# A four-layer graph network on one core: the rows between layers 1 and 2 are stored in another order, and the gathers of layer 3 get a small clear behind each

## The chip, the cores and the metric

The kernel runs on one core of one Trainium2 chip. The metric is the device time of one execution in microseconds (us), as the median of the runs shown. Engines are called PE (TensorE; PEld is its weight load), DVE (VectorE), ACT (ScalarE), POOL (GpSimd) and SP (the sync engine, which here only issues DMAs). L936 is line 936 of the kernel.

## What is computed

The graph has N = 2708 nodes with 128 features each, and a dense 2708 x 2708 matrix `adj` that is mostly zero (a row has some 16 entries). Four layers follow each other, each with a residual and a layer norm:

```
x = layernorm(x + (adj.T @ x) / adj.sum(axis=0))                    # layer 0
m = gelu(s[i] + d[j] + b);  agg[i] = sum_j adj[i, j] * m            # layer 1
x = layernorm(x + layernorm(gelu([x, agg] @ U.T + u) + x) * w + b)
h = adj @ (x @ W) + b                                               # layer 2
x = layernorm(x + leaky(gamma * batchnorm(h) + beta))
for each of 4 heads:                                                # layer 3
    s = exp(8 * tanh((leaky(x1[i] + x2[j]) @ a) / 8)) * adj
    out = leaky((s / s.sum(-1)) @ x @ Wlin.T)
x = layernorm(x + concat(out) @ w)
```

## The kernel before

The kernel works with lists of neighbours instead of the dense matrix. Nodes are taken in 22 blocks of 128 (21 full blocks and one of 20).

**Up to about 203 us.** SP loads the rows of `adj` into a ring of nine slots (`ring`, L338, tile `rows`, 10.8 KB in each partition). PE sums layer 0, DVE extracts each row's neighbours, and the rows are ranked by their number of neighbours. `rank[i]` is the place of node i in that order and `perm[r]` is the node at place r. Lists and layer-0 rows are written to DRAM in rank order by scatters on POOL (L255, an indirect DMA that takes its row numbers from a column of indices).

**Layer 1, about 203 to 1021 us.** The loop at L1035 takes the 22 blocks in rank order. `messages` (L865) gathers, for each neighbour slot of a block, 128 rows of 512 bytes from `d_dram` (`gather`, L247: one indirect DMA on POOL for each column of indices). Up to eight gathers fill one `msg` tile, of which there are five. DVE adds a term (L896), ACT applies gelu (L899) and DVE sums the weighted rows (L882, L884). `update` (L906) makes the block's new rows `x_n`; the last step of that is L321. Rows of a block lie in rank order, so L936 scatters them by `perm` into `x2_dram`, which is thereby in node order. Beside this, PE transposes `adj` into `at_dram` (L944, ACT L974, SP L976). From the twelfth block on, `layer2` (L1001) gathers 128 rows of `at_dram` by `perm` into a ring slot (tile `at_rows`, 1.35 MB each, L1005) and PE sums layer 2 (L1014, L1018).

**Between the layers, about 1021 to 1112 us.** The pools of layers 1 and 2, the ring among them, are closed at the end of the `with` at L337. The pools `ready` and `bn` (L1097, L1099) are then laid out in the same memory. SP loads `x2_dram` into the tile `x2` (L1103, L1104). DVE forms batch norm (L1121 to L1145), makes masks for layer 3 (`masks`, L1150, whose first instructions are iotas on POOL, L1147, L1155, L1157), and from L1185 on normalises; L1190 adds `x2`. The rows of the table `t2_dram` (644 floats a row) are written by SP.

**Layer 3, about 1112 to 1912 us.** Neighbour lists are cut into 100 groups of four columns ("quads"). `fetch` (L1531) gathers four times up to 128 rows of 2576 bytes from `t2_dram` into a tile `g4`, of which there are nine (`GOT`, L82). In each quad PE repeats and adds rows (L1358, L1364), DVE computes scores (L1556, L1557, L1374, L1382), and ACT sums them (L1390). Two quads are closed together (`rest`, L1395), and with PE's L1436 their `g4` tiles come free. Finished rows are scattered by POOL to the output (L1512). In this layer PE, DVE and ACT run in the order in which the code is written; POOL's and SP's order, and in layers 1 and 2 nearly everybody's, is set by a scheduler that works with estimated times. `tc.issue_after(i)` puts an instruction behind `i` in the order of its engine, without a wait.

Of the kernel before, what the change touches and what calls it, by code (L numbers as in the profile page):

```python
# [1 line left out]

# [7 lines left out]
FP = mybir.dt.float32  # L10
# [5 lines left out]
P = 128  # L16
N = 2708
D = 128
NFULL = N // P
NREM = N - NFULL * P  # L20
NBLK = NFULL + 1
# [7 lines left out]
I8 = mybir.dt.int8  # L29
# [30 lines left out]
RING = 9  # L60
LW = 2 * SLOTS + 2
BLOCKS = [(b * P, min(P, N - b * P)) for b in range(NBLK)]
# [23 lines left out]
def gnn_resnorm_kernel(  # L86
# [21 lines left out]
    nc = tc.nc  # L108
# [98 lines left out]
    keep = ctx.enter_context(tc.tile_pool(name="keep", bufs=1))  # L207
# [9 lines left out]
    x2_dram = tables.tile([NBLK * P, D], FP, name="x2_dram")  # L217
# [3 lines left out]
    t2_dram = tables.tile([NBLK * P, RW], FP, name="t2_dram")  # L221
    ls = keep.tile([P, NBLK, LW], FP, name="ls")
    idx = keep.tile([P, NBLK, SLOTS], I32, name="idx")
    perm = keep.tile([P, NBLK], I32, name="perm")
# [5 lines left out]
    idx3 = keep.tile([P, CHUNK3[NB3]], I32, name="idx3")  # L230
    val3 = keep.tile([P, CHUNK3[NB3]], FP, name="val3")
    rank = keep.tile([P, NBLK], I32, name="rank")
# [6 lines left out]
    ones = keep.tile([P, P], FP, name="ones")  # L239
    nc.gpsimd.memset(ones, 1.0)  # L240

    def natural(dram, b0, b1):

        return dram[b0 * P : b1 * P, :].rearrange("(b p) w -> p b w", p=P)

    def gather(dst, table, index):
        nc.gpsimd.indirect_dma_start(  # L247
            out=dst,
            out_offset=None,
            in_=table[0:N, :],  # L250
            in_offset=bass.IndirectOffsetOnAxis(ap=index, axis=0),
        )

    def scatter(table, index, rows):
        return nc.gpsimd.indirect_dma_start(  # L255
            out=table,
            out_offset=bass.IndirectOffsetOnAxis(ap=index, axis=0),
            in_=rows,
            in_offset=None,
        ).ins  # L260
# [69 lines left out]

    graph = ExitStack()
    own_ps = graph.enter_context(tc.tile_pool(name="own_ps", bufs=1, space=PSUM))

    def banks(name):
        return [bank.tile([P, 512], FP, name=f"{name}{i}", tag="bank") for i in range(6)]

    with ExitStack() as layer:  # L337
        ring = layer.enter_context(tc.tile_pool(name="ring", bufs=RING))  # L338
        work = layer.enter_context(tc.tile_pool(name="work", bufs=1))
        small = layer.enter_context(tc.tile_pool(name="small", bufs=2))  # L340
        engine = mybir.EngineType
# [312 lines left out]
        for g in KINDS:  # L654
            j = 32 // g
# [250 lines left out]
        def update(b, x_s, x_st, parts):  # L906
            n = BLOCKS[b][1]
            tp = tail_ps.tile([P, 512], FP, name="tail")
            for i in range(2):
                nc.tensor.matmul(  # L910
                    tp[:, 0:n], lhsT=parts[0:n, i, :], rhs=ident[0:n, 0:n],
                    start=(i == 0), stop=(i == 1),
                )
            x_b = mine.tile([P, D], FP, name="x_b")
            nc.vector.tensor_tensor(x_b[0:n], x_s[0:n, 1, :], lnb[0:n], ALU.add)
            agg_t = mine.tile([P, P], FP, name="agg_t")
            nc.scalar.copy(agg_t[:, 0:n], tp[:, 0:n])
            pn = tp[0:n, P : 2 * P]
            nc.tensor.matmul(pn, lhsT=x_st[:, 0:n], rhs=u1_t, start=True, stop=False)
            nc.tensor.matmul(pn, lhsT=ones[0:1, 0:n], rhs=updb[0:1, :], start=False, stop=False)  # L920
            nc.tensor.matmul(pn, lhsT=agg_t[:, 0:n], rhs=u2_t, start=False, stop=True)
            new = mine.tile([P, 1, D], FP, name="new")
            x_n = mine.tile([P, 1, D], FP, name="x_n")
            sums = mine.tile([P, 2], FP, name="sums1")
            h, s0, s1 = new[0:n, 0, :], sums[0:n, 0:1], sums[0:n, 1:2]
            nc.scalar.activation(h, pn, AF.Gelu)
            nc.vector.scalar_tensor_tensor(
                h, h, 1.0, x_s[0:n, 1, :], ALU.mult, ALU.add, accum_out=s0
            )
            rstd = deviation(mine, n, 1, new[0:n], s0)  # L930
            nc.vector.scalar_tensor_tensor(h, h, s0, lnw[0:n], ALU.add, ALU.mult)
            nc.vector.scalar_tensor_tensor(
                h, h, rstd[0:n, 0:1], x_b[0:n], ALU.mult, ALU.add, accum_out=s1
            )
            normalised(mine, n, 1, new[0:n], s1, x_n[0:n])
            scatter(x2_dram, perm[0:n, b : b + 1], x_n[0:n, 0, :])  # L936
            nc.tensor.transpose(tp[:, 256 : 256 + n], x_n[0:n, 0, :], ident[0:n, 0:n])
            x_nt = mine.tile([P, P], FP, name="x_nt")
            nc.scalar.copy(x_nt[:, 0:n], tp[:, 256 : 256 + n])
            px = tp[0:n, 384:512]  # L940
            nc.tensor.matmul(px, lhsT=x_nt[:, 0:n], rhs=w2_l2, start=True, stop=True)
            nc.scalar.copy(xw[0:n, b, :], px)
# [92 lines left out]
        for i, b in enumerate(TURNS):  # L1035
# [10 lines left out]
            for _ in range(2 if i < 1 else 1):  # L1046
                if left:
                    e = left.pop(0)
# [15 lines left out]
            for _ in range(2 if i in (9, 10, 11) else 1):  # L1064
                if i and again:
                    e = again.pop(0)
# [3 lines left out]
            if i >= 11:  # L1070
                for k in range(2 * (i - 11), min(i, 2 * (i - 10))):
                    layer2(k)
        layer2(NBLK - 1)

# [21 lines left out]
    with ExitStack() as layer:  # L1098
        work = layer.enter_context(tc.tile_pool(name="bn", bufs=1))  # L1099
        small = layer.enter_context(tc.tile_pool(name="bn_small", bufs=2))  # L1100
        hb = work.tile([P, NBLK, D], FP, name="hb")
        x2 = work.tile([P, NBLK, D], FP, name="x2")
        nc.sync.dma_start(x2[:, 0:NFULL, :], natural(x2_dram, 0, NFULL))  # L1103
        nc.sync.dma_start(x2[0:NREM, NFULL, :], x2_dram[NFULL * P : N, :])  # L1104
        a_all = keep.tile([P, HEADS, D], FP, name="a_all")
        nc.scalar.dma_start(a_all, att.partition_broadcast(P))
        w1_sb = keep.tile([P, HEADS, D], FP, name="w1_s")
# [75 lines left out]
        for b0, count, n in quads():  # L1183
            h = hb[0:n, b0 : b0 + count]
            nc.vector.tensor_tensor(h, h, broad(scale, n, count), ALU.mult)  # L1185
            nc.vector.tensor_tensor(h, h, broad(beta_row, n, count), ALU.add)
            nc.vector.scalar_tensor_tensor(h, h, 0.2, h, ALU.mult, ALU.max)
            sums = small.tile([P, 4], FP, name="sums2")
            for j in range(count):
                nc.vector.scalar_tensor_tensor(  # L1190
                    hb[0:n, b0 + j, :], hb[0:n, b0 + j, :], 1.0, x2[0:n, b0 + j, :],
                    ALU.mult, ALU.add, accum_out=sums[0:n, j : j + 1],
                )
            normalised(
                small, n, count, h, sums[0:n, 0:count], xs[0:n, b0 : b0 + count, :],
                newton=False,
            )
            w = (count - 1) * P + n
            nc.sync.dma_start(
                t2_dram[b0 * P : b0 * P + w, HD : HD + D].rearrange("(b p) w -> p b w", p=n),  # L1200
                xs[0:n, b0 : b0 + count, :],
            )
            for b in range(b0, b0 + count):
                did = scatter(x3_dram, rank[0:n, b : b + 1], xs[0:n, b, :])
                for before in sent:
                    tc.declare_no_dep(
                        did, before, query=mybir.DependencyQuery.ANY_SYNC,
                        reason="each row has a place of its own",
                    )
                sent.append(did)  # L1210
            pt = bank.tile([P, 512], FP, name="pt_x3", tag="bank")
            for j in range(count):
                nc.tensor.transpose(
                    pt[:, j * P : j * P + n], xs[0:n, b0 + j, :], ident[0:n, 0:n]
                )
            xt = small.tile([P, 512], FP, name="xt3")
            nc.scalar.copy(xt[:, 0:w], pt[:, 0:w])
            for j in range(count):
                at = slice(j * P, j * P + n)
                pm = bank.tile([P, 512], FP, name="pm_t", tag="bank")  # L1220
                nc.tensor.matmul(pm[0:n], lhsT=xt[:, at], rhs=w2_sb, start=True, stop=True)
                pa = bank.tile([P, 512], FP, name="pa_t", tag="bank")
                nc.tensor.matmul(
                    pa[0:n, 0:HEADS], lhsT=xt[:, at], rhs=w_a2, start=True, stop=True
                )
                row = small.tile([P, HD], FP, name="t_row", bufs=4)
                nc.scalar.copy(row[0:n], pm[0:n])
                beta_t = small.tile([P, HEADS], FP, name="beta_t", bufs=4)
                nc.vector.tensor_copy(beta_t[0:n], pa[0:n, 0:HEADS])
                r0 = (b0 + j) * P  # L1230
                nc.sync.dma_start(t2_dram[r0 : r0 + n, 0:HD], row[0:n, :])
                nc.sync.dma_start(t2_dram[r0 : r0 + n, HD + D : RW], beta_t[0:n, :])
# [6 lines left out]
    with ExitStack() as layer:  # L1239
# [291 lines left out]
        def fetch(i):  # L1531
            b, j = quads[i]
            e = BLOCKS3[b][0] * (P // BLOCKS3[b][0])
            g4 = got.tile([P, 4, RW], FP, name="g4")
            for r in range(4):
                ch = CHUNK3[b] + 4 * j + r
                gather(g4[0:e, r, :], t2_dram, idx3[0:e, ch : ch + 1])
            gathered[i] = g4

        fetch(0)  # L1540
# [1 line left out]
        for i, (b, j) in enumerate(quads):  # L1542
            g, jj = BLOCKS3[b]
            e = g * (P // g)
# [553 lines left out]
```

## Time and profile before

| what | us |
|---|---|
| median of 3 runs (lowest, highest) | 1938.81 (1932.17, 1943.18) |
| the profiled execution | 1931.8 |
| its span | 1930.1 |
| mean granted clock of PE, as a share of full speed | 0.72 |

| engine | busy us | share of the span |
|---|---|---|
| PE | 1260.2 | 65% |
| DVE | 1110.4 | 58% |
| POOL | 895.3 | 46% |
| PEld | 859.7 | 45% |
| ACT | 825.7 | 43% |

The profile is of one execution of the kernel. A line of its page or its views names a line of the code, an engine, an operation, and the tiles written and read (`out<-in`, buffer numbers left out, so `x2_dram` and `x3_dram` are both shown as `x_dram`, `t2_dram` as `t_dram`). Times in brackets are idle time of the engine before the instruction and what ended it; "issue" means that the engine waited for nothing that the profile shows, and "remote" that the releaser is not recorded. The view of busy time by stretch gives, for each stretch, the busy time of each engine with its number of instructions, then PE's granted clock, the busy share of the DMA engines and what they moved in GB/s. A POOL gather is busy while it issues; its data land later.

### The profile page before, as it was taken

The page shows a single profiled execution, that of the slowest core. Times are in us where ns is not written, and L with a number is a line of the kernel's source. Part 1 is how long each engine was busy: PE and PEld are TensorE (multiplying, and loading weights), DVE is VectorE, ACT ScalarE, POOL GpSimd, SP SyncE. Part 2 cuts the span into 40 slices and gives each one's busy share as a digit, 9 for nine tenths or more (in the row PEclk, how much of TensorE's full clock was granted, in tenths as well). Part 3 has the DMA queues.
Part 4 walks back from the last instruction along what each step waited for, and adds up shares of the span by engine and source line. Part 5 has one row for each costly group of instructions (what it writes and reads, how often), then busy time and mean ns, then how long its engine had stood idle before and what let it go on. Part 6 is the DMA issues. An engine that isn't in the chain of part 4 may idle for free. (4 is left out here: it accounts for less than half of the span.)

```text
span 1930.1 us, 24100 instructions
## 1 busy us (share of the span) xinstructions
PE 1260.2 (65%) x5971; PEld 859.7 (45%) x5971; DVE 1110.4 (58%) x4643; ACT 825.7 (43%) x3508; POOL 895.3 (46%) x1003
## 2 busy tenths in 40 slices
PE   7973312363446453564673738888888889878884
PEld 7973212342335442553663314444444545444553
DVE  8997545674535422433446416665666667566663
ACT  3565435543323210211112415665565567455663
POOL 1004754445643366444330464664555556545530
PEclk8995655555555676776766867888787888788785
DMA  8642555675535524223231574775565565756530
GB/s 285 238 148 75 138 146 163 174 193 166 143 99 145 175 44 159 95 92 142 80 112 40 167 242 120 205 203 151 165 197 170 167 189 153 195 154 182 175 109 7
DMA packets 167678, 289.66 MB, mean 150 GB/s; under 512 B 49600, under 2 KB 121502, under 8 KB 160429
## 3 DMA queue, kind: packets, MB, share of 16 engines
q0 software_dynamic: 60496, 190.77, 34.1%
q1 hardware_dynamic: 99489, 92.57, 15.7%
q10 hardware_dynamic: 7544, 4.69, 1.0%
q8 instruction: 50, 0.82, 0.2%
q14 instruction: 99, 0.81, 0.1%
HBM read 242.51 MB, written 45.36 MB: 149 GB/s over the span
## 5 line engine op out<-in xcount | busy, mean ns | idle before, releaser
L247 POOL DMA_INDIRECT g<-t_dram,idx x400 | 399.9, 1000 | 314.1 <-issue 188.6
L247 POOL DMA_INDIRECT msg<-d_dram,idx x368 | 349.5, 950 | 260.1 <-issue 170.1
L1390 ACT ACTIVATE sum_junk<-g 126x128 bf16<-126x128 f32 (+3 forms) x1200 | 353.1, 296 | 78.4 <-ACT sum_junk L1390 46.8
L1364 PE MATMUL z<-g,ident 126*126 126x512 f32 (+3 forms) x400 | 251.3, 760 | 0.0
L1358 PE MATMUL z<-x,copies 32*126 32x512 f32 (+3 forms) x800 | 209.0, 765 | 48.2 <-DVE g L1557 19.0
L1390 ACT ACTIVATION_READ_ACCUMULATOR sum_junk<-g 126x1 f32 (+3 forms) x1200 | 225.3, 188 | 0.0
L969 PE MATMUL pt_a<-ident,rows 128*128 128x128 f32 (+2 forms) x475 | 116.8, 404 | 141.6 <-ACT at_sb L974 84.6
L1018 PE MATMUL acc<-x_nat,at_rows 128*128 128x128 f32 (+2 forms) x968 | 157.7, 324 | 50.8 <-issue 31.3
L1018 PEld LDWEIGHTS acc<-x_nat,at_rows 128*128 128x128 f32 (+2 forms) x968 | 142.4, 230 | 62.3 <-issue 39.0
L969 PEld LDWEIGHTS pt_a<-ident,rows 128*128 128x128 f32 (+2 forms) x475 | 85.7, 210 | 163.9 <-ACT at_sb L974 99.3
L1364 PEld LDWEIGHTS z<-g,ident 126*126 126x126 f32 (+3 forms) x400 | 83.0, 231 | 165.4 <-issue 160.2
L1436 PE MATMUL po_s<-wm,g 126*128 126x24 f32 (+6 forms) x800 | 114.8, 297 | 51.3 <-DVE wm L1423 49.3
L884 DVE SCALAR_TENSOR_TENSOR own<-msg,ls,own 128x128 f32<-128x128 f32 (+1 forms) x302 | 105.7, 350 | 73.9 <-ACT msg L899 28.2
L420 PE MATMUL acc<-x_nat,rows 128*128 128x129 f32 (+3 forms) x1012 | 130.5, 291 | 24.9 <-DMA rows<-in_adj_dram 14.0
L1556 DVE TENSOR_TENSOR g<-g,z 126x1024 f32<-126x1024 f32 (+3 forms) x100 | 121.5, 1215 | 34.0 <-remote 13.9
L1436 PEld LDWEIGHTS po_s<-wm,g 126*128 126x128 f32 (+3 forms) x800 | 111.7, 221 | 62.9 <-DVE wm L1423 54.0
L420 PEld LDWEIGHTS acc<-x_nat,rows 128*128 128x128 f32 (+2 forms) x1012 | 124.8, 200 | 30.1 <-DMA rows<-in_adj_dram 14.7
L1382 DVE SCALAR_TENSOR_TENSOR g<-g,a_ps 126x1024 f32<-126x1024 f32 (+3 forms) x100 | 121.2, 1212 | 0.0
L1374 DVE SCALAR_TENSOR_TENSOR g<-z,a 126x128 f32<-126x128 f32 (+3 forms) x400 | 91.7, 285 | 27.4 <-issue 8.1
L899 ACT ACTIVATE msg<-msg 128x896 f32<-128x896 f32 (+4 forms) x55 | 50.4, 916 | 131.8 <-DVE msg L896 106.3
L1358 PEld LDWEIGHTS z<-x,copies 32*126 32x126 f32 (+3 forms) x800 | 63.0, 211 | 96.2 <-issue 45.5
L1557 DVE SCALAR_TENSOR_TENSOR g<-z,a 126x512 f32<-126x512 f32 (+3 forms) x100 | 68.6, 686 | 54.0 <-remote 25.5
(301 smaller groups left out, 2106.5 us busy)
## 6 DMA issues: line engine op xcount, KB each, us to landing
rows<-in_adj_dram SPq DMA_DIRECT2D x34, 1354.0 KB
at_dram<-at_sb SPq DMA_DIRECT2D x105, 256.0 KB
g<-t_dram,idx POOLq DMA_INDIRECT x400
msg<-d_dram,idx POOLq DMA_INDIRECT x368
t_dram<-t_row SPq DMA_DIRECT2D x21, 256.0 KB
x_s<-dx_dram SPq DMA_DIRECT2D x21, 128.0 KB
at_dram<-at_sb SPq DMA_DIRECT2D x21, 64.0 KB
t_dram<-x_nat SPq DMA_DIRECT2D x5, 256.0 KB
```

Of the source, the lines that this page charges most:

```text
L247: nc.gpsimd.indirect_dma_start(out=dst, out_offset=None, in_=table[0:N, :], in_offset=bass.IndirectOffsetOnAxis(ap=index, axis=0),)
L420: nc.tensor.matmul(accs0[k][0:m, c0 : c0 + f1 - f0], lhsT=rows[0:n, j0 : j0 + m], rhs=x_nat[0:n, b, f0:f1], start=k not in started, stop=( ...
L884: nc.vector.scalar_tensor_tensor(to, m, v, last, ALU.mult, ALU.add)
L969: nc.tensor.transpose(pt[0:m, j, 0:n], rows[0:n, c0 : c0 + m], ident[0:n, 0:n])
L1018: nc.tensor.matmul(accs2[ib // 4][0:m, (ib % 4) * D : (ib % 4 + 1) * D], lhsT=at[0:n, i0 : i0 + m], rhs=xw[0:n, b, :], start=(k == 0 and i ...
L1358: nc.tensor.matmul(z2[0:e, r, :] if r < 2 else zs[r - 2][0:e], lhsT=copies[g][rows, j, :], rhs=own[b][1][rows, :], start=True, stop=r < 2, ...
L1364: nc.tensor.matmul(zs[r - 2][0:e], lhsT=ident[0:e, 0:e], rhs=g4[0:e, r, 0:HD], start=False, stop=True, skip_group_check=True,)
L1374: nc.vector.scalar_tensor_tensor(g4[0:e, r, part_of], z[0:e, part_of], 0.0, a[0:e, part_of], ALU.max, ALU.mult, accum_out=sc[0:e, hd : hd ...
L1382: nc.vector.scalar_tensor_tensor(z, z, 0.0, a_ps[0:e].unsqueeze(1).to_broadcast((e, 2, HD)), ALU.max, ALU.mult)
L1390: nc.scalar.activation(junk[0:e], g4[0:e, r, hd * D : (hd + 1) * D], AF.Identity, accum_out=sc[0:e, r, hd : hd + 1],)
L1436: nc.tensor.matmul(po[:, p0 * HEADS : (p0 + g) * HEADS], lhsT=g4s[i][0:e, r, HD : HD + D], rhs=wm[0:e, 4 * i + r, :, :], start=True, stop= ...
L1556: nc.vector.tensor_tensor(z, z, z2[0:e], ALU.add)
```

## The change

Three things are changed.

1. `x2_dram` is kept in rank order. The scatter by `perm` on POOL becomes a plain store on SP's queue.
2. Layer 2's residual still needs `x2` in node order, so it is gathered by `rank` in 22 indirect DMAs on POOL at the end of the layer-2 loop, into two slots of the ring (21 blocks in one, the last block in the other). The two loads on SP and the tile `x2` go. For this the ring is opened at the right end of the memory and stays until layer 3 begins.
3. Each gather of layer 3 is followed on POOL by a clear (memset) of 200 bytes in one partition, and the next gather is put behind that clear. The gathers of layers 1 and 2 and of `x2` have none.

```diff
+    pause = keep.tile([1, 200], I8, name="pause")
...
     def gather(dst, table, index):
-        nc.gpsimd.indirect_dma_start(
+        return nc.gpsimd.indirect_dma_start(
...
+    paused = {}
+
+    def gather_spaced(dst, table, index):
+        before = paused.get(table.name)
+        with tc.issue_after(before) if before is not None else nullcontext():
+            did = gather(dst, table, index)
+        with tc.issue_after(did.ins):
+            paused[table.name] = nc.gpsimd.memset(pause, 0).ins
...
+    ring = graph.enter_context(tc.tile_pool(name="ring", bufs=RING, side="right"))
...
-        ring = layer.enter_context(tc.tile_pool(name="ring", bufs=RING))
...
-            scatter(x2_dram, perm[0:n, b : b + 1], x_n[0:n, 0, :])
+            nc.sync.dma_start(x2_dram[b * P : b * P + n, :], x_n[0:n, 0, :])
...
         layer2(NBLK - 1)
+        x2_full = ring.tile([P, N], FP, name="x2_full", tag="rows")
+        x2_last = ring.tile([P, N], FP, name="x2_last", tag="rows")
+        x2 = [x2_full[:, b * P : b * P + D] for b in range(NFULL)] + [x2_last[:, 0:D]]
+        for b in range(NBLK):
+            n = BLOCKS[b][1]
+            gather(x2[b][0:n, :], x2_dram, rank[0:n, b : b + 1])
...
-        x2 = work.tile([P, NBLK, D], FP, name="x2")
-        nc.sync.dma_start(x2[:, 0:NFULL, :], natural(x2_dram, 0, NFULL))
-        nc.sync.dma_start(x2[0:NREM, NFULL, :], x2_dram[NFULL * P : N, :])
...
-                    hb[0:n, b0 + j, :], hb[0:n, b0 + j, :], 1.0, x2[0:n, b0 + j, :],
+                    hb[0:n, b0 + j, :], hb[0:n, b0 + j, :], 1.0, x2[b0 + j][0:n, :],
...
-                gather(g4[0:e, r, :], t2_dram, idx3[0:e, ch : ch + 1])
+                gather_spaced(g4[0:e, r, :], t2_dram, idx3[0:e, ch : ch + 1])
```

More of the change, by code (lines that the diff above doesn't have):

```diff
@@ L1 @@
-from contextlib import ExitStack, contextmanager
+from contextlib import ExitStack, contextmanager, nullcontext
 import concourse.bass as bass
```

## The prediction

> **What bounds the kernel now.** I read the page's busy times first: no engine is busy for more than 65% of the span, so waits set the time. Then the waits of POOL and the busy time by stretch. POOL's waits between 640 and 1030 us, by line (us in total, times, longest):
>
> ```profile
> POOL msg L247 <- issue: 71.6, 147, 14.8
> POOL x_dram L255 <- DVE x_n L321: 67.8, 6, 17.0
> POOL x_dram L255 <- DVE own L884: 47.0, 5, 12.6
> POOL x_dram L255 <- DVE spread L618: 15.0, 1, 15.0
> ```
>
> The last three rows, 130 us, are the scatter of L936 waiting for `x_n` at the head of POOL's queue, with gathers behind it. But those gathers are not what layer 1 waits for: in DVE's waits of the same stretch no row names a landed `msg`, and in the timelines the last gather of a block's last `msg` tile ends 17 to 41 us before DVE has summed it (the fourteenth block: 723.1 and 746.9). What costs time is seen in the busy time by stretch while POOL issues without a pause (us; PE, PEld, DVE, ACT, POOL, clock, DMA share, GB/s):
>
> ```profile
> 744.00:748.00 4.00, 2.70 (x22) 2.18 (x20) 2.73 (x8) 0.00 (x0) 2.96 (x4) 1.00 0.17 49
> 748.00:752.00 4.00, 0.00 (x0) 0.00 (x0) 0.00 (x0) 0.00 (x0) 3.08 (x4) 0.80 0.18 49
> 752.00:756.00 4.00, 0.00 (x0) 0.00 (x0) 0.00 (x0) 0.00 (x0) 3.08 (x4) 0.50 0.27 65
> ...
> 768.00:772.00 4.00, 0.00 (x0) 0.00 (x0) 0.00 (x0) 0.00 (x0) 3.08 (x4) 0.50 0.18 50
> ...
> 780.00:784.00 4.00, 3.52 (x11) 2.63 (x12) 0.40 (x3) 0.71 (x3) 0.00 (x0) 0.50 0.00 0
> ```
>
> POOL's run of indirect DMAs began at 739.06 and ended at 775.1. From 748 on, 9 us into it, PE, DVE and ACT do next to nothing (a few instructions about 765), with the DMA engines some 20% busy in these rows; some 4 us after its end they go on. Layer 3 begins alike: its first 36 gathers run from 1114.5 to 1160.
>
> ```profile
> 1130.00:1140.00 10.00, 2.07 (x4) 0.50 (x4) 1.22 (x1) 1.21 (x6) 7.56 (x9) 0.63 0.84 263
> 1140.00:1150.00 10.00, 0.01 (x1) 0.00 (x0) 0.00 (x0) 0.00 (x0) 7.56 (x9) 0.50 0.83 265
> ...
> 1170.00:1180.00 10.00, 10.00 (x28) 4.17 (x24) 7.62 (x19) 8.84 (x51) 0.00 (x0) 0.65 0.00 1
> 1180.00:1190.00 10.00, 10.00 (x55) 5.79 (x55) 9.70 (x38) 7.58 (x50) 7.06 (x6) 1.00 0.46 106
> ```
>
> So long unbroken runs of indirect DMAs on POOL stop the other engines. What the path of it is, the trace does not show. Over the 76 stretches of 10 us from 1120 to 1880, DVE is busy 4.54 us on average where POOL is busy 7.2 or more (13 of them), 6.48 where POOL is busy 6 to 7.2 (19). In layers 1 and 2 (200 to 1020) it is 3.56 (32 stretches) against 5.17 where POOL is at 4 to 6.
>
> **The change, part by part.** Against the profiled execution, 1931.8 us.
>
> *The scatter becomes a store on SP.* 22 scatters of 0.99 us and 0.30 us between two leave POOL: 28.4 us. The first ten stand where POOL waits for free `msg` tiles anyway (rows of 3 to 18 us idle before the next gather): 0. The other twelve, from 675 on, stand in or before runs that stop the others: 12 x 1.29 = 15.5. The 130 us of waiting behind the queue's head I cost at nothing, because gathers are early already; if they were not, it would be -130. Nothing (cover complete) and -28 are the near ends. I take **-15**. On SP the store waits for `x_n`, and the load of the next block's own rows (L857) may stand behind it; L857 itself already waits 216 us in total for DVE L927 of the same update, and L321 follows L927 by 12.8 us (783.06, 795.90). The load is issued a block ahead and a block takes 25 to 40 us, which hides it; without that cover it is up to 12 x 12.8 = 154.
>
> *The 22 gathers of x2.* No such run stands between the layers now. The timelines of SP and DVE:
>
> ```profile
> 1030.50 0.80 SPq L1103 DMA_DIRECT2D x<-x_dram  x1
> 1031.36 3.00 SPq L1104 DMA_DIRECT2D x<-x_dram  x1
> ```
>
> ```profile
> 1053.20 0.29 DVE L1190 SCALAR_TENSOR_TENSOR hb<-hb,x 128x128 f32<-128x128 f32 x1
> ```
>
> The gathers can begin when the last `x_n` (done at 1020.7) has landed, about 1022.5, and take 22 x 1.25 = 27.5 us, to 1050; DVE wants the first block at 1053 and the last some 20 us later, so the data are in time. But it is a run as long as that of 739. Past its first 9 us, 18.5 us of it lie on a stretch where DVE is busy 17.1 of 20 us (1030 to 1050). By the ratio of 3.56 to 5.17 a third goes, 6 us; if all stops, 18.5. I take **+12**. Zero is the end if the scheduler spreads them.
>
> *The ring stays at the right.* POOL's first iota waited 8.56 us for PE L1018 because `ready` lay on the ring, and DVE stood idle 9.8 us before 1030.46; masks (some 11 us of DVE) could now move there. But the iotas may stand behind the 22 gathers. Between 0 and -9.8: I take **-2**.
>
> *The clears.* The nearest rows are POOL instructions between two indirect DMAs:
>
> ```profile
> 1084.39 0.98 POOL L255 DMA_INDIRECT x_dram<-x_nat,rank  x1 [0.30 <-DVE beta_t L1229]
> 1085.39 0.27 POOL L1155 IOTA row_of<- 128x126 int32 x1
> 1085.60 0.15 POOL L1157 IOTA start<- 128x9 int32 x1
> 1085.93 0.98 POOL L255 DMA_INDIRECT x_dram<-x_nat,rank  x1 [0.17 <-issue]
> ```
>
> Two iotas of 0.42 us lengthen the step from 1.27 to 1.54 us, since they use the gap. Memsets here take 0.096 us (one column) to 0.42 (396 columns); 128 columns of floats take 0.20. So one clear of 200 bytes, 0.13 to 0.26 us, adds 0 to 0.2 us to a step of 1.25; I take 0.1. POOL then needs 4 x 1.35 = 5.4 us a quad where a quad takes 7.7 (766 us for 100), so its own time is hidden; if not, 400 x 0.1 = 40. POOL's share in a run falls from 76% to 70%, and the space between two gathers grows from 0.30 to 0.40. That moves the 13 full stretches to where the 19 are: 13 x 10 x (1 - 4.54/6.48) = 39 us. Two quads take 12.6 us at their lower quartile and 15.3 on average (start to start of every second L1556), so everything above that floor is 50 x 2.7 = 136 us, the far end; +40 the other, if a run only gets longer. I take three quarters of 39: **-30**.
>
> Sum: -15 + 12 - 2 - 30 = -35, so 1896.8 on the profiled execution. That one stands 7.0 below the median of the runs (1938.81), so against the median I say **1904**.
>
> **Rivals.** About 0.5%, 9.7 us, is what a measurement of this kernel can tell from no change.
>
> - *Layer 3 is set free.* If short spaces are enough for what is held up to get through, runs of eight gathers (10 us, against 9 us until the stop at 739) no longer stop anybody, and the first 36 do not either: -136 in place of -30, some 1798; half of it, 1866. For it: in the fastest pairs PE, DVE and ACT keep their pace beside eight gathers. Against: others make no progress in the 0.30 us that are there now. [...] Chance 0.12.
> - *The clears do nothing.* If the others stand for as long as gathers are issued, whatever lies between them, and POOL has room, layer 3 stays: -5, 1934. Chance 0.15.
> - *Slower: the runs only get longer.* The stop lasts as long as POOL's run does. Place: 1023 to 1054, where a run of 22 is new, and each run of eight in layer 3, now 0.8 us longer. Price: 18.5 + 50 x 0.8 = 58, less 15 and 2: +41, 1980; half of that, 1959. With no relief in layer 3 the other terms come to +1.5, so it decides from (9.7 - 1.5)/400 = 0.02 us added to a gather on. For it: with POOL at 6.87 of 10 there is a stretch with DVE at 2.75 (from 1330). Against: the 19 such stretches average 6.48. Chance 0.22.
> - *Slower: the clear shuts DVE out.* If a memset on POOL held what DVE needs, 400 x 0.13 to 0.26 = 52 to 104 us, DVE being busy 64%, would give +33 to +67: about 1984 with the rest at -5. DVE's L1382 takes 1.21 us with a gather beside it (1435.55) and without (1430.53), which speaks against it for gathers; a memset beside DVE is not in the trace. [...] Chance 0.06.
>
> Forecast 0.45, by itself 1866 to 1929. Faster by over 0.5%: 0.45 + 0.12 = 0.57; within: 0.15; slower: 0.28. The range 1840 to 1985 leaves out about half of the first rival and a part of the slower ones.
>
> **What would show it.** Right: POOL's timeline has a memset behind each L247 of layer 3 and steps of 1.3 to 1.45 us; stretches from 1130 to 1160 with DVE above 2 of 10 us; layer 3 (first to last L1556) below 766 us by about 30; no L255 on `x_n`, and layer 1 ends some 15 us earlier; from the last L321 to L1190 about 12 us more than 32.9. Wrong: the same 766 us, or more, with POOL at 7 of 10 and DVE at 4; SP's L857 late, so that DVE L887 waits for it; or a stretch after 1023 that grows by far more than 18 us.

## The result, and the profile after

The changed kernel takes 1917.98 us (median of 4 runs, 1915.76 to 1920.61) beside 1938.09 for the kernel before: a ratio of 0.9907, 95% interval 0.9879 to 0.9936. A later, larger set (lower down as `after_again`; 12 runs, of which the ratio leaves out one slow one) gave 0.9927 (0.9892 to 0.9961). The change is worth some 14 to 20 us.

The profiled execution took 1915.8 us, its span 1914.0. Cut at three marks that both traces have (end of the last `x_n` of layer 1; first and last add of z, L1556 before and L1570 now):

| stretch, us | before | after | difference |
|---|---|---|---|
| start to the last `x_n` | 1020.7 | 1016.7 | -4.0 |
| last `x_n` to the first add of z | 101.1 | 120.5 | +19.4 |
| first to last add of z (layer 3) | 766.0 | 732.7 | -33.3 |
| rest | 42.3 | 44.1 | +1.8 |
| span | 1930.1 | 1914.0 | -16.1 |

So a gain of 37 us is half given back between the layers.

**Layer 3.** The costliest groups of the changed kernel, gathers and clears (busy time, mean ns of one, then idle time before them):

```profile
L249 POOL DMA_INDIRECT g<-t_dram,idx x400 | 404.0, 1010 | 172.5 <-issue 115.9
L263 POOL MEMSET pause<- 1x200 int8 x400 | 102.3, 256 | 0.1
```

A clear takes 0.256 us and starts as the gather ends. The timeline of POOL shows what that does to the step (start, duration):

```profile
1149.95 0.95 POOL L249 DMA_INDIRECT g<-t_dram,idx  x1 [0.16 <-issue]
1150.90 0.26 POOL L263 MEMSET pause<- 1x200 int8 x1
1151.32 0.95 POOL L249 DMA_INDIRECT g<-t_dram,idx  x1 [0.16 <-issue]
```

The step from gather to gather is 1.37 us where it was 1.25. Half of the clear lies in the gap that was there already, so it adds 0.12. The busy time by stretch at the beginning of layer 3, where the first 36 gathers run from 1123.8 to 1173.9 (before: from 1114.5 to 1160):

```profile
1130.00:1140.00 10.00, 8.81 (x25) 3.89 (x27) 4.07 (x10) 1.23 (x4) 8.87 (x16) 0.61 0.84 265
1140.00:1150.00 10.00, 5.73 (x20) 2.03 (x14) 3.14 (x10) 3.88 (x25) 8.70 (x16) 0.91 0.80 242
1150.00:1160.00 10.00, 3.99 (x4) 0.99 (x4) 1.62 (x9) 0.00 (x0) 8.87 (x15) 0.50 0.80 242
```

Counted from the first gather, the row from 1140 stands beside the one from 1130 of before (16 us into the run): DVE gets 3.14 us where it had 1.22. The row from 1150 stands beside the one from 1140 of before (26 us in): 1.62 where it had 0.00. The DMA engines are about as busy as they were (0.80, and 0.83 to 0.84 before). It is a relief, not a cure: from 1150 to 1160 ACT still does nothing.

**Layer 1.** POOL's waits between 640 and 1030 us, the first three rows:

```profile
POOL msg L249 <- issue: 109.7, 141, 14.7
POOL row_of L1169 <- DVE rs_y L282: 52.7, 1, 52.7
POOL x_full L249 <- PE tail L952: 17.0, 1, 17.0
```

The scatters that waited 130 us for `x_n` are gone, and the last message gather now ends at 946.3 instead of 991.5. Layer 1 ends only 4 us earlier all the same. The long runs are still there (us; PE, PEld, DVE, ACT, POOL, clock, DMA share, GB/s):

```profile
744.00:748.00 4.00, 0.00 (x0) 0.00 (x0) 0.00 (x0) 0.00 (x0) 3.08 (x4) 0.50 0.51 133
748.00:752.00 4.00, 0.00 (x0) 0.00 (x0) 0.00 (x0) 0.00 (x0) 3.08 (x4) 0.50 0.99 406
```

**Between the layers.** The 22 gathers of `x2` run from 1019.1 to 1047.3 in steps of 1.25 us. DVE's waits from 1030 to 1060:

```profile
DVE first L1173 <- issue: 14.7, 1, 14.7
DVE bn_scale L1156 <- PE ps_v L1146: 4.3, 1, 4.3
```

`first` reads `jrow`, whose iota POOL issues at 1047.35, behind the gathers. PE is held as well: its sums for the variance (`ps_v`) let DVE go on at 1052.5, where before it was 1040.1.

### The profile page after: what moved, and what is told of

Same layout as the page of the kernel before. It is cut to its first block, busy times and chain, and to the rows that moved or that the text cites. A ratio compares the mean times of both kernels' runs of the same rounds, so it can differ in the third digit from the quotient of the medians.

```text
span 1914.0 us, 24560 instructions
## 1 busy us (share of the span) xinstructions
PE 1266.4 (66%) x5971; PEld 869.4 (45%) x5971; DVE 1108.5 (58%) x4643; ACT 821.2 (43%) x3508; POOL 1000.6 (52%) x1403
## 5 line engine op out<-in xcount | busy, mean ns | idle before, releaser
L249 POOL DMA_INDIRECT g<-t_dram,idx x400 | 404.0, 1010 | 172.5 <-issue 115.9
L1372 PE MATMUL z<-x,copies 32*126 32x512 f32 (+3 forms) x800 | 198.3, 752 | 34.9 <-issue 22.5
L980 PE MATMUL pt_a<-ident,rows 128*128 128x128 f32 (+2 forms) x475 | 112.8, 395 | 154.2 <-ACT at_sb L985 105.2
L1029 PE MATMUL acc<-x_nat,at_rows 128*128 128x128 f32 (+2 forms) x968 | 173.9, 340 | 26.6 <-issue 21.1
L1029 PEld LDWEIGHTS acc<-x_nat,at_rows 128*128 128x128 f32 (+2 forms) x968 | 154.3, 243 | 42.5 <-issue 39.9
L431 PE MATMUL acc<-x_nat,rows 128*128 128x129 f32 (+3 forms) x1012 | 127.9, 287 | 26.5 <-DMA rows<-in_adj_dram 15.3
L1570 DVE TENSOR_TENSOR g<-g,z 126x1024 f32<-126x1024 f32 (+3 forms) x100 | 121.5, 1215 | 38.5 <-PE z L1372 11.3
L263 POOL MEMSET pause<- 1x200 int8 x400 | 102.3, 256 | 0.1
L456 DVE FIND_INDEX8 ci<-cv,rows 128x8 uint32<-128x247 f32 (+2 forms) x242 | 98.8, 408 | 0.0
L1571 DVE SCALAR_TENSOR_TENSOR g<-z,a 126x512 f32<-126x512 f32 (+3 forms) x100 | 68.7, 687 | 49.8 <-remote 15.3
```

The costliest lines, as they stand in the source:

```text
L249: return nc.gpsimd.indirect_dma_start(out=dst, out_offset=None, in_=table[0:N, :], in_offset=bass.IndirectOffsetOnAxis(ap=index, axis=0),)
L263: paused[table.name] = nc.gpsimd.memset(pause, 0).ins
L431: nc.tensor.matmul(accs0[k][0:m, c0 : c0 + f1 - f0], lhsT=rows[0:n, j0 : j0 + m], rhs=x_nat[0:n, b, f0:f1], start=k not in started, stop=( ...
L980: nc.tensor.transpose(pt[0:m, j, 0:n], rows[0:n, c0 : c0 + m], ident[0:n, 0:n])
L1029: nc.tensor.matmul(accs2[ib // 4][0:m, (ib % 4) * D : (ib % 4 + 1) * D], lhsT=at[0:n, i0 : i0 + m], rhs=xw[0:n, b, :], start=(k == 0 and i ...
L1372: nc.tensor.matmul(z2[0:e, r, :] if r < 2 else zs[r - 2][0:e], lhsT=copies[g][rows, j, :], rhs=own[b][1][rows, :], start=True, stop=r < 2, ...
```

## The experiments

Stages are from one profiled execution each, times from all runs. "Between" is last `x_n` to first add of z, "layer 3" is first to last add of z.

| kernel | last `x_n` | between | layer 3 | ratio to before (95%) |
|---|---|---|---|---|
| before | 1020.7 | 101.1 | 766.0 | 1 |
| changed | 1016.7 | 120.5 | 732.7 | 0.9907 (0.9879 to 0.9936) |
| after_again | 1013.4 | 118.4 | 737.4 | 0.9927 (0.9892 to 0.9961) |
| clears_only | 1026.5 | 97.5 | 758.9 | 0.9915 (0.9888 to 0.9943) |
| no_clears | 1017.9 | 117.4 | 768.0 | 1.0073 (1.0042 to 1.0104) |
| jrow_first | 1022.8 | 118.6 | 741.8 | 0.9917 (0.9887 to 0.9946) |
| x2_spaced | 1016.2 | 114.6 | 733.3 | 0.9900 (0.9866 to 0.9935) |
| all_spaced | 988.0 | 116.5 | 749.2 | 0.9805 (0.9763 to 0.9848) |
| clears_right | 1022.5 | 99.3 | 753.9 | 0.9845 (0.9811 to 0.9879) |
| every_4th | 1006.0 | 122.5 | 702.4 | 0.9742 (0.9703 to 0.9781) |
| every_4th_all_scatter | 950.6 | 100.4 | 709.5 | 0.9270 (0.9230 to 0.9310) |
| every_4th_all | 873.7 | 107.5 | 703.1 | 0.8900 (0.8863 to 0.8937) |

The theory on record: long runs of gathers stop the other engines, and the space that a clear makes lets them through. The first rival: the clears do nothing and the time goes and comes by the new order of the work. The second: the clear or the gather shuts DVE out of something both need.

**The parts, one at a time.** `clears_only` is the kernel before with the third change alone:

```diff
-                gather(g4[0:e, r, :], t2_dram, idx3[0:e, ch : ch + 1])
+                gather_spaced(g4[0:e, r, :], t2_dram, idx3[0:e, ch : ch + 1])
```

> The kernel before with the clears of layer 3 alone (scatter and the two loads of x2 stay). If space between gathers lets the other engines through: layer 3 (first to last add of z) falls from 766 to about 733 us, as in the changed kernel, the rest stays, and the time is some 33 us below the kernel before: 1902 to 1910. If the clears do nothing and the 33 us came with the new order of the work: layer 3 stays at 766 and the time at 1938.

Measured: 1922.64 beside 1940.04, 17 us less. This is faster, but by half of what was expected, and layer 3 in its trace took 759 us. `no_clears` is the changed kernel with that line turned back.

> The changed kernel without the clears: the store on SP and the 22 gathers of x2 remain. If the clears are worth 33 us: layer 3 at about 766 us and the time 13 to 16 us above the kernel before, 1951 to 1954 (layer 1 some 4 us shorter, the stretch between the layers 19 us longer). If they do nothing: 1918, as the changed kernel.

Measured: 1954.24 beside 1940.04, 14 us more, with layer 3 at 768. That is the first theory's number. Without the clears the change is slower than the kernel it replaces: store and gathers cost 14 us, and the clears bring 1.5 to 1.7% (ratios 0.9927 and 0.9907 against 1.0073), 28 to 32 us. So a clear behind each gather is worth 17 us in the kernel before and 28 to 32 us beside the store; the intervals of the ratios are too wide to say that the two differ.

**Layer 3 with and without the store.** To find why the clears alone left layer 3 at 759, `clears_right` adds the ring at the right end of the memory to them:

```diff
+    ring = graph.enter_context(tc.tile_pool(name="ring", bufs=RING, side="right"))
...
-        ring = layer.enter_context(tc.tile_pool(name="ring", bufs=RING))
```

> The kernel before with the clears of layer 3 and the ring at the right end of the memory (scatter and loads of x2 stay). In the kernel with the clears alone layer 3 took 759 us where the changed kernel takes 733, with the same order of instructions. If the place of the tiles in memory makes this: layer 3 at 733 to 743, the time 1895 to 1910. If it is chance of one execution: the time is that of the clears alone, 1917 to 1927.

Measured: 1904.85 beside 1932.56, but layer 3 took 754 us in its trace, and that one execution was the slowest of its six (1920.47). So the time is the first expectation's, and layer 3 is not. The order of POOL's, DVE's and ACT's work in layer 3 is the same in all kernels with one clear behind each gather, from the first gather on; in the kernels without clears or with groups of them, a scatter to the output stands at most one gather from there. With one clear behind each gather, layer 3 took 733, 737, 742 and 733 us in four executions with the store, 759 and 754 with the scatter, 749 in `all_spaced`. What makes these 20 us, and whether the ring's place is worth the 0.7% between the ratios of `clears_only` and `clears_right` (some 13 us, from two sets of runs on two chips), stays open.

**Between the layers.** Two ways to take away one of the two suspects. `jrow_first` makes the iota ahead of the gathers:

```diff
+        jrow = keep.tile([P, 8], I32, name="jrow")
+        counted = nc.gpsimd.iota(jrow, pattern=[[1, 8]], base=0, channel_multiplier=0)
...
-            gather(x2[b][0:n, :], x2_dram, rank[0:n, b : b + 1])
+            with tc.issue_after(counted.ins):
+                gather(x2[b][0:n, :], x2_dram, rank[0:n, b : b + 1])
```

> The changed kernel with the first iota of the masks (jrow) ahead of the 22 gathers of x2 on POOL. If DVE's 14.7 us of idle time at 1033 to 1047 is only the wait for that iota: DVE makes the first masks in that time, and everything from there on is 7 to 10 us earlier, about 1909. If the run of gathers itself stops the engines: DVE still gets little done until the run ends, and the time stays within 4 us of the changed kernel, 1914 to 1920.

`x2_spaced` puts a clear behind each of the 22 gathers:

```diff
-            gather(x2[b][0:n, :], x2_dram, rank[0:n, b : b + 1])
+            gather_spaced(x2[b][0:n, :], x2_dram, rank[0:n, b : b + 1])
```

> The changed kernel with a clear behind each of the 22 gathers of x2 as well. If the run of gathers stops the engines: PE finishes the sums for the variance, which now end at about 1052, up to 10 us earlier, and the time falls by 3 to 10 us, 1908 to 1915. If only POOL's order costs (the iota behind the gathers): the gathers end 22 x 0.12 = 2.6 us later and the time rises by as much, to about 1921.

Measured: 1925.88 and 1920.40, both beside 1940.04; neither ratio can be told from the changed kernel's. The stretch is 118.6 and 114.6 us long. DVE's waits say why. In `jrow_first`, from 1035 to 1066:

```profile
DVE bn_scale L1159 <- PE ps_v L1149: 21.2, 1, 21.2
```

In `x2_spaced`, from 1030 to 1056:

```profile
DVE first L1173 <- issue: 12.7, 1, 12.7
DVE bn_scale L1156 <- PE ps_v L1146: 2.6, 1, 2.6
```

With the iota early, DVE makes its masks and then stands 21.2 us for PE, which the run holds. With the run spaced, PE is done at 1035 and DVE stands 12.7 us for the iota. By time, both runs came out near the second expectation, without a gain. By the trace, both suspects were guilty, each behind the other, and taking one away shows the other.

**A bench for the disputed cost.** `handoff` holds no graph network: twelve stretches of gathers, each beside a chain of small instructions.

```diff
+        for k in range(80):
+            nc.vector.tensor_scalar(t, u, 1.0, None, ALU.add)
+            nc.scalar.copy(u, t)
```

> No part of the graph network is computed (the output is a copy of x): twelve stretches with a barrier between them, each with up to 40 gathers of 128 rows on POOL and beside them a chain of 80 round trips of small instructions on DVE and ACT (or PE and DVE), or 240 instructions of DVE alone; a clear of 200, 20 or 800 bytes behind each gather, or one of 800 behind each fourth. If a run of gathers stops what passes from one engine to another, and space lets it through: the chain beside 40 plain gathers makes next to no progress from some 10 us after the run's start to its end, with a clear of 200 bytes it goes on at a third of its own pace or better, and longer clears are better still; DVE alone, which waits for nobody, keeps its pace of 0.2 us an instruction. If DVE itself is shut out: DVE alone stops as well, and PE's chain is no different. If clears work only as a lower rate of gathers: one long clear behind each fourth gather is worth as much as one behind each.

Measured in one execution, us for a round trip of DVE and ACT: 0.51 alone, 0.87 beside plain gathers (from 10 us after the run's start to its end). As a mean over all 80 trips: 0.77 with plain gathers, 0.70 with clears of 20 bytes, 0.54 with 200, 0.62 with 800, 0.61 with 800 behind each fourth gather. Longer clears were not better still, as the first theory had it. With clears and no gathers the mean is 0.53, but the 40 clears were over after 12 us; beside them a trip took 0.62. This chain was slowed, not stopped.

Its mean hides two phases. Beside plain gathers, trips of 0.51 and 0.74 us take turns for 29 us; from 30 us into the run to its end most take 1.40 us. With clears of 20 bytes the trips of 1.40 begin at 25 us, with clears of 200 none comes in the 43 us of the chain. DVE alone was not spared as the first theory expected. For 17 us its instructions follow each other at once; then they stand apart, though each still takes 0.20 us. From 10 us into the run to its end that is 0.70 us an instruction, where it is 0.23 undisturbed (`x7` is seven in a row, idle time is in brackets):

```profile
447.91 1.72 DVE L149 TENSOR_SCALAR t<-t 128x64 f32<-128x64 f32 x7
...
454.27 1.10 DVE L149 TENSOR_SCALAR t<-t 128x64 f32<-128x64 f32 x4 [1.21 <-DVE t L149]
456.39 0.20 DVE L149 TENSOR_SCALAR t<-t 128x64 f32<-128x64 f32 x1 [1.01 <-DVE t L149]
457.79 0.43 DVE L149 TENSOR_SCALAR t<-t 128x64 f32<-128x64 f32 x2 [1.20 <-issue]
```

So the first theory's words, what passes from one engine to another, are too narrow: here DVE waits for no other engine and stands all the same. That DVE is shut out does not fit either, since its instructions keep their length. And PE with DVE fared worst: 2.83 us a round trip, 1.43 with a clear behind each gather, 1.08 after the run.

A second, smaller loss is in the first phase of the chain of DVE and ACT. The timeline in the stretch with plain gathers:

```profile
140.70 0.94 POOL L136 DMA_INDIRECT got<-narrow_dram,idx  x1 [0.30 <-issue]
...
141.24 0.43 DVE L145 TENSOR_SCALAR t<-u 128x64 f32<-128x64 f32 x1 [0.31 <-ACT u L146]
...
141.95 0.95 POOL L136 DMA_INDIRECT got<-narrow_dram,idx  x1 [0.30 <-issue]
141.97 0.20 DVE L145 TENSOR_SCALAR t<-u 128x64 f32<-128x64 f32 x1 [0.31 <-issue]
```

The DVE instruction that falls into the end of a gather (141.64) takes 0.43 us, the one at its beginning 0.20. Beside clears without gathers:

```profile
640.00 3.06 POOL L142 MEMSET pause<- 1x200 int8 x10
...
640.31 0.31 DVE L145 TENSOR_SCALAR t<-u 128x64 f32<-128x64 f32 x1 [0.31 <-ACT u L146]
```

It takes 0.31 us: a clear lengthens it by 0.11. The instruction at 141.97 lies wholly inside a gather of 0.95 us and takes its usual 0.20. What makes the 0.43 and the 0.31, the trace does not show.

**A clear behind every gather.** `all_spaced` uses `gather_spaced` for the messages, the rows of layer 2 and `x2`, too.

> The changed kernel with a clear behind every gather (messages of layer 1 and the rows for layer 2, too). If space lets others through in layer 1 as in layer 3: the stop of 748 to 780 us goes and layer 1 ends 10 to 25 us earlier, 1895 to 1910. If runs only get longer there: layer 1 ends later by up to 480 x 0.12 = 58 us less what POOL waits anyway, 1920 to 1950.

Measured: 1895.03 beside 1932.56. Layer 1 ended at 988.0, 29 us earlier, a little more than the first theory's 10 to 25 us. But the stops are fewer, not gone. Of the stretches of 10 us from 200 to 870 us in which POOL is busy 7.2 us or more, DVE is busy under 1.5 us in 3 of 40, where it was 7 of 22 in the changed kernel; and one that is left is as deep as those were (us; PE, PEld, DVE, ACT, POOL, clock, DMA share, GB/s):

```profile
802.00:812.00 10.00, 0.00 (x0) 0.00 (x0) 0.00 (x0) 0.00 (x0) 8.87 (x15) 0.66 0.21 51
```

**The same clears, four at a time.** `every_4th` has the 400 clears of the changed kernel in groups:

```diff
-        with tc.issue_after(did.ins):
-            paused[table.name] = nc.gpsimd.memset(pause, 0).ins
+        paused[table.name] = did.ins
+        made[0] += 1
+        for _ in range(4 if made[0] % 4 == 0 else 0):
+            with tc.issue_after(paused[table.name]):
+                paused[table.name] = nc.gpsimd.memset(pause, 0).ins
```

> The changed kernel with four clears behind each fourth gather of layer 3 in place of one behind each: as many clears, the same mean rate of gathers. If any pause in a run lets through what is held up, or only the rate counts: layer 3 stays at 733 to 743 us, the time at 1915 to 1926. If each gather needs its own space: layer 3 goes back towards 768, the time to 1940 to 1955.

Measured: 1879.21 beside 1932.56, layer 3 at 702 us. Neither expectation was met: it is better than one behind each, by 30 to 35 us in layer 3. At the start of layer 3 (first gather at 1114.7) the others now keep working:

```profile
1130.00:1140.00 10.00, 10.00 (x39) 4.04 (x38) 9.47 (x33) 8.03 (x51) 8.01 (x15) 1.00 0.77 230
1140.00:1150.00 10.00, 9.57 (x26) 3.84 (x23) 8.07 (x23) 8.83 (x52) 7.91 (x12) 0.83 0.73 208
```

From the first to the tenth add of z it takes 52 us, where the changed kernel takes 70 and the kernel before 86. The step from gather to gather is longer, too: 1.52 us on average over the first 36, against 1.40 and 1.28. POOL's timeline shows why:

```profile
1301.15 0.98 POOL L249 DMA_INDIRECT g<-t_dram,idx  x1 [0.30 <-issue]
1302.43 0.98 POOL L249 DMA_INDIRECT g<-t_dram,idx  x1 [0.30 <-issue]
1303.41 1.19 POOL L266 MEMSET pause<- 1x200 int8 x4
1305.20 1.00 POOL L249 DMA_INDIRECT g<-t_dram,idx  x1 [0.60 <-ACT sum_junk L1407]
```

Only the first of four clears falls into the gap that a gather leaves anyway, so the group really costs time (0.60 of the 2.77 us from 1302.43 to 1305.20 are a wait for ACT): the "same mean rate" of the expectation was wrong.

**The bench with PE.** `handoff_pe` asks how much of that is needed, with round trips between PE and DVE beside 48 gathers. It is one execution, too.

> No part of the graph network is computed (the output is a copy of x): eleven stretches, each with 48 gathers on POOL (rows of 512 or 2576 bytes) and beside them 80 round trips between PE and DVE; clears of 200 bytes: none, one or two behind each gather, four behind each fourth, eight behind each eighth. In the stretch with plain gathers of the earlier test such a round trip took 2.83 us, with one clear behind each 1.43, without gathers 1.08. If one longer space frees the handoffs better than four short ones (as layer 3 at 702 us says): 1.1 to 1.3 us with four behind each fourth. If only the share of time without gathers counts: 1.4, as with one behind each, and less with two. If the gain of layer 3 has another cause: four behind each fourth is worse than one behind each, 1.6 to 2.8.

| gathers of 128 rows, clears of 200 bytes | mean step (first to last gather), us | us a round trip, from 10 us into the run: rows of 512 bytes | of 2576 bytes |
|---|---|---|---|
| no gathers | | 1.01 | |
| plain | 1.25 | 2.93 | 3.11 |
| one behind each | 1.37 | 1.72 | 1.54 |
| four behind each fourth | 1.50 | 1.01 | 1.01 |
| eight behind each eighth | 1.50 | 1.01 | 1.01 |
| two behind each | 1.70 | 1.01 | |

Groups of four do better than the 1.1 to 1.3 us of the first expectation.

In the first 10 us of every run there are 9 or 10 round trips, as without gathers. The means from there on again mix two phases. From PE's end (which the profile models) to DVE's start it is 0.04 us without gathers. Beside plain gathers it stays at that for 17 to 18 us of the run, then grows from trip to trip to 4.63 (once 5.33, just after the last gather), and is back at 0.04 some 7 to 9 us after the last gather. With one clear behind each it stays at 0.04 for 28 to 33 us and is then mostly between 1.1 and 1.9. With groups, or with two behind each, it does not grow in these runs of 73 to 82 us. DVE's timeline in the plain run (gathers from 164.63 to 224.51):

```profile
182.71 0.23 DVE L144 COPY t<-acc 128x64 f32<-128x64 f32 x1 [0.78 <-PE acc L143]
185.18 0.23 DVE L144 COPY t<-acc 128x64 f32<-128x64 f32 x1 [2.25 <-PE acc L143]
...
197.11 0.23 DVE L144 COPY t<-acc 128x64 f32<-128x64 f32 x1 [4.68 <-issue]
202.71 0.23 DVE L144 COPY t<-acc 128x64 f32<-128x64 f32 x1 [5.38 <-remote]
...
231.41 0.23 DVE L144 COPY t<-acc 128x64 f32<-128x64 f32 x1 [1.18 <-PE acc L143]
232.42 0.23 DVE L144 COPY t<-acc 128x64 f32<-128x64 f32 x1 [0.78 <-PE acc L143]
```

The busy time by stretch (here without ACT: PE, PEld, DVE, POOL, clock, DMA share, GB/s), in the order plain, one behind each, four behind each fourth, and the same three with rows of 2576 bytes:

```profile
190.00:200.00 10.00, 1.38 (x4) 1.00 (x4) 0.45 (x2) 7.56 (x9) 1.00 0.21 52
310.00:320.00 10.00, 3.67 (x12) 2.73 (x12) 1.35 (x6) 8.86 (x15) 1.00 0.19 49
430.00:440.00 10.00, 6.83 (x21) 5.02 (x20) 2.25 (x10) 7.86 (x14) 1.00 0.18 46
...
660.00:670.00 10.00, 0.69 (x2) 0.50 (x2) 0.34 (x2) 7.58 (x8) 1.00 0.89 265
790.00:800.00 10.00, 3.69 (x12) 2.56 (x11) 1.12 (x5) 8.86 (x15) 1.00 0.83 241
880.00:890.00 10.00, 6.83 (x21) 4.96 (x21) 2.25 (x10) 7.97 (x15) 1.00 0.77 227
```

Five times the bytes change little, and POOL's busy share does not order the rows: 7.56 is the worst, 7.86 is free, 8.86 lies between. What orders them in these runs is how many gathers start in a given time; a long space is not needed, since two clears behind each gather are free as well (1.01 us a round trip). From 1.37 to 1.50 us a gather, the price goes from 52 to 70% of a round trip (1.54 and 1.72 against 1.01) to nothing, in runs of 48 gathers. Where the time is lost, in the plain run:

```profile
202.99 0.69 PE L143 MATMUL acc<-t,w 128*128 128x64 f32 x2 [4.91 <-DVE t L144]
...
208.32 0.23 DVE L144 COPY t<-acc 128x64 f32<-128x64 f32 x1 [5.38 <-remote]
...
208.60 0.69 PE L143 MATMUL acc<-t,w 128*128 128x64 f32 x2 [4.92 <-issue]
```

PE and DVE take their usual 0.69 and 0.23 us. From DVE's end (208.55) to PE's start it is 0.05 us, from PE's modelled end (203.68) to DVE's start 4.6.

**All gathers in groups, with the store and with the scatter.** `every_4th_all` counts to four for each table and uses `gather_spaced` everywhere. `every_4th_all_scatter` does the same to `clears_right`.

> The changed kernel with four clears behind each fourth gather of every table (messages, rows for layer 2, x2, layer 3). If the two gains add up (layer 1 ended some 28 us earlier with a clear behind every gather, layer 3 is some 30 us shorter with four behind each fourth): 1850 to 1865. If layer 1 needs a space behind each gather: 1875 to 1885.

> The same clears in the kernel with the scatter of x2 on POOL and the loads of x2 on SP, the ring at the right. If the store and the 22 gathers cost more than they bring (19 us between the layers against 4 in layer 1): 10 to 15 us below the last one, 1838 to 1855. If the store is worth the 15 us that were predicted: the same time or slower by up to 3 us.

Measured: 1726.78 and 1801.24 beside 1937.23. Both expectations are far off, on the good side, and the order of the two is reversed. `every_4th_all` is 11% faster than the kernel before (ratio 0.8900, 0.8863 to 0.8937): the best version here. Layer 1 ends at 873.7 us, 143 us earlier than in the changed kernel. Its page has POOL busier than ever:

```profile
PE 1215.3 (70%) x5971; PEld 841.9 (49%) x5971; DVE 1114.3 (65%) x4643; ACT 821.4 (48%) x3508; POOL 1103.4 (64%) x1811
```

Over the stretches of 10 us from 200 to 870 us in which POOL is busy 7.2 us or more, DVE is busy 5.71 us on average (51 stretches, 3 of them under 1.5); in the changed kernel 3.51 (22), in the kernel before 3.77 (29).

One rival was not tested. In layers 1 and 2 other clears also give another order of work: in `every_4th_all` the 22 gathers of `at_rows` stand in fours behind 221 to 360 message gathers, in the changed kernel mostly in pairs behind 222 to 368, and PE's order differs as well. No run there changes the spaces and keeps the order, so how the 143 us divide between the two is open. In layer 3, where the order stays, the spaces alone remain.

The store, with its 22 gathers, now decides 74.5 us. In the scatter version POOL's waits (560 to 970 us) are led by

```profile
POOL x_dram L269 <- DVE x_n L335: 92.9, 7, 16.5
```

and DVE's by

```profile
DVE msg L910 <- DMA msg<-d_dram,idx: 86.9, 16, 10.4
```

With the store, no row of DVE's waits names a landed message, and these lead:

```profile
DVE own L896 <- ACT msg L913: 25.1, 4, 10.4
DVE new L941 <- ACT new L940: 23.9, 9, 7.1
```

**The changed kernel again**, for a firmer ratio:

> The changed kernel itself beside the others on one chip. By the runs so far: ratio to the kernel before 0.985 to 0.993; layer 3 between 730 and 760 us, since kernels with the same order in it gave 733 to 759.

Measured: 1921.64 beside 1937.23, layer 3 at 737; both lie in the ranges.

## Why the prediction came out as it did

The forecast of 1904 was 14 us below the 1918 measured. The sum of -35 became -16 in the two traces and -14 to -20 by the medians: one term came out in size, two were off.

- **What bounds the kernel: right.** Runs of indirect DMAs do stop the others; the bench shows it by itself (a round trip of 1.01 us takes 2.93 from 10 us into the run). The "9 us into it" is of that place in this kernel; in the benches the first 17 to 30 us of a plain run are free of the stop.
- **The clears, -30: right in size, in part by luck.** Layer 3 fell by 33.3 us; by the ratios the clears are worth 28 to 32 beside the store, but 17 alone. The step was put at 1.35 us and is 1.37. The size came from averages over stretches, of which three quarters were taken; in the trace 15.5 of the 33.3 us were won before the tenth add of z, on the nine quads of the first long run. The reason was incomplete: "the space between two gathers grows from 0.30 to 0.40" was taken as what frees the others. In the bench a step of 1.25 us stops them after 17 to 18 us of a run, one of 1.37 later and by less (after 28 to 33 us; 1.72 us a round trip in place of 2.93), and one of 1.50 not at all in runs of 73 to 82 us (1.01). (Two quads took 15.5 us, start to start, and not 15.3, which moves only the far end.)
- **The store, -15: mis-sized.** The last `x_n` came 4 us earlier. Over single executions it stood at 1006.0 to 1022.8 with the store and untouched message gathers (six), at 1020.7 to 1026.5 with the scatter (three): the means are 8 us apart. The step that failed is that each scatter taken out of a run shortens the stop by its 1.29 us; the runs that stop layer 1 stayed, and the last message gather ended 45 us earlier for a gain of 4.
- **The 130 us behind the queue's head at nothing: right here, by a condition.** The text said that gathers are early already. In the kernels with groups of clears everywhere they no longer are, and the scatter costs 74.5 us. The bound of -130 was the one to keep in mind.
- **SP's queue: the cover held.** L868 still waits behind L938, but DVE's waits for the block's own rows (`x_s`) are 25 us between 640 and 1030, where they were 34.
- **The 22 gathers and the ring, +12 and -2: mis-sized, +19.4.** The first gather began 2.4 us behind the last `x_n` (1016.7 to 1019.1), where the text put 1.8, an estimate that no row of before shows. "By the ratio of 3.56 to 5.17 a third goes" failed: DVE stood for 14.7 us, and PE was late too. The masks could not fill the time, since the iota stood behind the gathers, as the text feared.
- **Rivals.** *Layer 3 is set free* did not happen with a step of 1.37; with groups of four layer 3 is at 702 us, 64 below before, about the half of 136 that was named. Its condition, that short spaces let through what is held up, was met in the bench at a step of 1.50 us (1.01 us a round trip), and at 1.37 only in part (1.54 and 1.72 in place of 3.11 and 2.93). *The clears do nothing* and *the runs only get longer* fall with `no_clears`. *The clear shuts DVE out* is real in small (0.11 us where a clear and a DVE instruction meet; its sum assumed the whole clear, 0.13 to 0.26) and does not decide.

Left open: what is held up in a run, and on which path; why layer 3 differs by 20 us among kernels with one order; what part of the gain in layer 1 is the scheduler's order; and whether the mean step alone decides or also the shape, since no single clear behind each gather was tried at 1.50.

## What to carry to other kernels

Read what other engines do *while* an engine issues many small DMAs, not only what that engine's queue waits for: here a stop that lay on everybody hid the other waits, and the change that takes such a wait away (the store) showed its worth (74.5 us) only with the stop mostly gone (DVE under 1.5 us in 3 of 51 busy stretches, in place of 7 of 22). Where gathers of 128 rows stop the others, try slowing them to the 1.50 us that was enough here in runs of 48, for every table and not one alone (1879.21 us with layer 3 alone, 1726.78 with all). Short clears one by one were half lost here in the gap that is there; in groups they were not (mean steps at the start of layer 3: 1.28 us without clears, 1.40 one by one, 1.52 in fours). Measure past the first 30 us of a run: in the benches the stop came after 17 to 30 us of plain gathers, and a shorter test would not have seen it. Try the parts of a change one by one: this one held a part worth 17 to 32 us and a pair that cost 14, and the pair was worth 74.5 in better company.

## What the hardware showed that was not expected

- Slower issue, with the order of work that came with it, made the kernel faster: by 136 us with the scatter, by 210 with the store, where POOL spent 208 us more busy time (895.3 to 1103.4).
- The price goes by the number of gathers, not by bytes: 512 and 2576 bytes a row cost a round trip of PE and DVE 2.93 and 3.11 us.
- The first part of a run is free of the long waits: 17 to 18 us for PE with DVE and for DVE alone, 29 for DVE with ACT, 28 to 33 for PE with DVE at a step of 1.37 us. Then the waits grow from trip to trip and outlast the last gather by up to 9 us, and at a step of 1.50 us they do not come in runs of 73 to 82 us. Why, the traces do not show.
- By the end of a plain run PE's news to DVE was 4.6 us late while DVE's news to PE took 0.05. DVE stood as well when it followed only itself, in multiples of some 0.70 us (an instruction each 0.70, 1.40 or 2.10).
